# First tile of x in two loads, the mask fill behind the third tile, one more weight cast on ScalarE

## The chip, the cores and the metric

The kernel runs on one core of one Trainium2 chip. The metric is the device time of one execution in microseconds (us). Times inside the kernel come from one profiled execution; they are counted from the first instruction of the program on the core.

The engines are named as the profile names them: PE is TensorE (PEld its weight loads), DVE is VectorE, ACT is ScalarE, POOL is GpSimd and SP is SyncE, which here only issues loads and stores.

## What is computed

A graph attention layer on 384 nodes with 1024 features, and a quantised gated feed-forward network (FFN) behind it, both with a layer norm in front and a residual around:

```python
def _layernorm(x, axis=-1, eps=1e-05):
    m = jnp.mean(x, axis=axis, keepdims=True)
    v = jnp.var(x, axis=axis, keepdims=True)
    return (x - m) / jnp.sqrt(v + eps)
...
q = x @ wq.T + bq                       # the same for k and v, 1024 x 1024 each
q2 = (q @ wiq.T + biq).reshape(N, H, D).transpose(1, 0, 2)    # 16 heads of 64, the same for k2, v2
mask = _build_mask(edge_index, edge_type, edge_type_weights, x.dtype)   # -inf where no edge
scores = jnp.einsum('hnd,hmd->hnm', q2, k2) * scale + mask[None]
attn = jax.nn.softmax(scores, axis=-1)
out = jnp.einsum('hnm,hmd->hnd', attn, v2)
return out.transpose(1, 0, 2).reshape(N, OUT_F) @ wo.T + bo
...
def _weight_fake_quant(w):
    scale = jnp.max(jnp.abs(w), axis=1, keepdims=True) / QMAX
    return jnp.clip(_ste_round(w / scale), -QMAX - 1.0, QMAX) * scale
gate = jnp.einsum('bsh,ih->bsi', xq, _weight_fake_quant(w_gate))
up = jnp.einsum('bsh,ih->bsi', xq, _weight_fake_quant(w_up))
h = _act_fake_quant(jax.nn.silu(gate) * up, clip_down[0])
return jnp.einsum('bsi,hi->bsh', h, _weight_fake_quant(w_down))
...
x = x + gnn(_layernorm(x))
x = x + ffn(_layernorm(x))
```

The FFN has 352 inner units, so w_gate and w_up are 352 x 1024 and w_down is 1024 x 352.

## The kernel before

The 384 rows of x are three tiles of 128 (NT = 3), the 1024 features eight chunks of 128 (KC = 8). The matrix work is in 32-bit floats but for the FFN, whose quantised weights and inputs are exact in bf16.

**Order of the work.** PE, SP and POOL run their instructions in the order of the program text in the whole kernel. DVE and ACT do so in the first stage (line 280) and in the last (line 791); between them, in the attention stage, a scheduler sets their order when the kernel is compiled. Every engine works through its own list in order: an instruction that waits holds up all that is behind it.

**Start (lines 84 to 382).** SP issues the loads: tiles 0 and 1 of x (line 88), the first two blocks of wq (line 80), tile 2 of x, then further blocks of wq, wk and so on, one 512 KB load each. Weight blocks go into eight buffers, and each load also waits for the landing of the eighth load before it. PE begins with 36 transposes of a unit matrix (WARM, line 328) that nobody reads. For each tile t of x:

- `row_stats(t)` on DVE: two statistics of 512 columns (line 294), their merger (295), and the reciprocal of the standard deviation (lines 122 to 131, with a square root on ACT),
- `normalise(t)` on DVE: two halves of 512 columns (line 302),
- `turn(t, xn, g)` on PE: four transposes for each half (line 311), copied out of PSUM by ACT in pairs (line 315),
- `q_first(o, t)` on PE: the products of tile t with the first two blocks of wq (line 320), as soon as the chunks are there.

In the text the work runs: statistics, normalisation and turning of tile 0; then statistics and normalisation of tile 1; `q_first(0, 0)`, then part of `q_first(1, 0)`; turning of tile 1, and so on to tile 2.

**POOL at the start.** It makes the unit matrix, issues the loads of biases, edge weights, clip factors and edges, makes two index tables (lines 109 and 112), clears `w_scale` (149), and fills the mask, 128 x 3 x 384 floats, with the value that stands for "no edge" (151). Once DVE has made the edge keys (345), POOL writes them to DRAM (348) and issues three loads that spread them over all partitions (271). Later DVE puts the diagonal into the mask (411), POOL writes the mask to DRAM (415), and 51 indirect transfers put the edges in (450). Line 464 loads the finished mask back.

**Projections (lines 480 to 513).** Each pair of weight blocks takes seven products of four matmuls (`project2`, Strassen's scheme in Winograd's form), from about 22 to 159 us. The last inner products for k (`inner_k`) use the same function in the attention stage.

**Attention stage (lines 709 to 787).** For each of eight pairs of heads p: score products (line 651) with the mask added on DVE (657) and the exponential on ACT (661), the weighting of the pair before (`weigh`: transposes on line 681 into two PSUM buffers, copies by ACT on line 683, products on line 689), and, spread between them, filler products: `inner_v` (line 625) for even p, `inner_k` (line 203) for odd p. In `project2` a product goes into one of two PSUM buffers (pool `ps_mm`), and a buffer is free for the next product but one when DVE and ACT have read it (lines 217 to 238).

**FFN weights.** Into the same stage `ffn_weights` spreads the quantisation of 14 blocks of FFN weights (u = 0 to 13): three of w_gate, three of w_up, eight of w_down. For each block: the largest value of each row (527) and its reciprocal scale (528, 530) on DVE, scaling to 8-bit integers on ACT (533, one buffer `w8b`), a cast to bf16 into `wqi` (two buffers), then transposes on PE (570 or 580) and a copy on ACT. The cast is on ACT (537) for blocks u < 3 and on DVE (539) for the others. PE transposes into the same two PSUM buffers (`ps_tp`) as `weigh`. Block u = 3, the first of w_up, is quantised during pair p = 1, while `inner_k(2)` is the filler.

**End (from line 839).** Output projection, residual, layer norm, FFN and the stores.

Of the kernel before, what the change touches and what calls it, by code (L numbers as in the profile page):

```python
# [32 lines left out]
P = 128  # L33
N = 384
NT = N // P
F = 1024
# [18 lines left out]
NO_EDGE = -8e30  # L55


def row_bcast(ap, n):
    return bass.AP(tensor=ap.tensor, offset=ap.offset, ap=[[0, P], [1, n]])
# [3 lines left out]
def gnn_ffn_kernel(ctx: ExitStack, tc: tile.TileContext, a: dict, out: bass.AP):  # L63
    nc = tc.nc
# [13 lines left out]
    def load_w(name, j):  # L78
        wt = w.tile([P, F], F32, name="wt")
        nc.sync.dma_start(wt, a[name][j])  # L80
        return wt


    x = act.tile([P, NT, F], F32, name="actT")
    for t in range(NT):
        if t == NT - 1:
            wq_first = [load_w("wq", o) for o in range(FIRST)]
        nc.sync.dma_start(x[:, t, :], a["x"][t * P : (t + 1) * P, :])
    bias_rows = const.tile([5 * KC, P], F32)
    etw = const.tile([P, 4], F32)  # L90
    clip = const.tile([P, 2], F32)
# [55 lines left out]
    w_scale = ffn.tile([P, 2, 3], F32)  # L147
    wd_scale = ffn.tile([P, KC], F32)
    nc.gpsimd.memset(w_scale, 0.0)
    mask = ffn.tile([P, NT, N], F32)  # L150
    nc.gpsimd.memset(mask, NO_EDGE)
    sig = ffn.tile([P, 2], F32)
    per_max = ffn.tile([P, 5], F32)

# [105 lines left out]
    with ph1_stack:  # L260
# [6 lines left out]
        def load_keys():  # L267
            c0 = len(key_b) * 4 * GROUP
            part = ph1.tile([P, 4 * GROUP * P], F32, name="key_b", bufs=3)
            n = min(4 * GROUP, EC - c0) * P  # L270
            nc.gpsimd.dma_start(part[:, :n], row_bcast(key_row_d[:, c0 * P : c0 * P + n], n))
            key_b.append(part)
# [25 lines left out]
        def normalise(t):  # L298
            xn = rows_p.tile([P, F], F32, name="row")
            for j in range(2):  # L300
                hs = slice(j * 512, (j + 1) * 512)
                nc.vector.tensor_scalar(
                    xn[:, hs], x[:, t, hs], mv1[:, t, 0:1], rstd1[:, t : t + 1], op0=ALU.subtract, op1=ALU.mult
                )
            return xn
# [11 lines left out]
        def q_first(o, t, ks=range(KC)):  # L317
            ts = slice(t * P, (t + 1) * P)
            for k in ks:
                nc.tensor.matmul(  # L320
                    pm_first[o][:, ts], wq_first[o][:, k * P : (k + 1) * P], xnT[:, k, ts],
                    start=(k == 0), stop=(k == KC - 1),
                )
# [24 lines left out]
        nc.gpsimd.dma_start(key_row_d.rearrange("a (c p) -> (a c) p", p=P), key_row)  # L348
        for _ in range(3):
            load_keys()  # L350
        xn = normalise(2)
        q_first(0, 1)
        q_first(1, 1, range(6))
# [171 lines left out]
    def quantise_rows(wn, rows, n, scale, on_scalar=False, wq=None):  # L525
        mx = small.tile([P, 1], F32, name="wmx")
        nc.vector.tensor_reduce(mx[:rows], wn[:rows, :n], axis=AX.X, op=ALU.max, apply_absolute_value=True)
        nc.vector.tensor_scalar(scale, mx[:rows], 1.0 / QMAX, None, op0=ALU.mult)
        rs = small.tile([P, 1], F32, name="wrs")
        nc.vector.reciprocal(rs[:rows], scale)  # L530

        w8b = rows_p.tile([P, F], I8, name="w8b", bufs=1)
        nc.scalar.activation(w8b[:rows, :n], wn[:rows, :n], AF.Copy, scale=rs[:rows])
        if wq is None:
            wq = rows_p.tile([P, F], BF16, name="wqi", bufs=2)
        if on_scalar:
            nc.scalar.copy(wq[:rows, :n], w8b[:rows, :n])
        else:
            nc.vector.tensor_copy(wq[:rows, :n], w8b[:rows, :n])
        return wq  # L540

    def ffn_weights():

        units = [(name, m, ic) for m, name in enumerate(("L0_ffn_w_gate", "L0_ffn_w_up")) for ic in range(3)]
        units += [("L0_ffn_w_down", 2, c) for c in range(KC)]
        ahead = []

        def load_row():
            name, m, j = units[len(ahead)]
            i0, rows = ICS[j] if m < 2 else (j * P, P)  # L550
            wn = rows_p.tile([P, F], F32, name="row")
            nc.sync.dma_start(wn[:rows, : F if m < 2 else I], a[name][i0 : i0 + rows, :])
            ahead.append(wn)

        load_row()
        load_row()
        yield
        for u, (name, m, j) in enumerate(units):
            wn = ahead[u]
            if len(ahead) < len(units):  # L560
                load_row()
            if m < 2:
                i0, rows = ICS[j]
                wT = (wgT, wuT)[m]

                wq = quantise_rows(wn, rows, F, w_scale[:rows, m, j : j + 1], on_scalar=u < 3)
                yield
                pt = ps_tp.tile([P, KC, P], BF16, name="tp")
                for k in range(KC):
                    nc.tensor.transpose(pt[:, k, :rows], wq[:rows, k * P : (k + 1) * P], ident_b[:rows, :rows])  # L570
                nc.scalar.copy(wT[:, :, i0 : i0 + rows], pt[:, :, :rows])
            elif j >= KC - LATE:
                quantise_rows(wn, P, I, wd_scale[:, j : j + 1], wq=wd_late[:, j - KC + LATE, :])
                yield
            else:
                wq = quantise_rows(wn, P, I, wd_scale[:, j : j + 1])
                yield
                pt = ps_tp.tile([P, 3, P], BF16, name="tp")
                for ic, (i0, rows) in enumerate(ICS):
                    nc.tensor.transpose(pt[:rows, ic, :], wq[:, i0 : i0 + rows], ident_b)  # L580
                nc.scalar.copy(wdT[:, 0:2, j * P : (j + 1) * P], pt[:, 0:2, :])
                nc.scalar.copy(wdT[:96, 2, j * P : (j + 1) * P], pt[:96, 2, :])

    prep = ffn_weights()

    next(prep)
    nc.sync.dma_start(biv_b, row_bcast(a["L0_gnn_biv"], F))

    with ExitStack() as ph:
# [124 lines left out]
        for p in range(NP):  # L714
# [12 lines left out]
            if p == NP - 2:  # L727

                x = act.tile([P, NT, F], F32, name="actT")
# [143 lines left out]
    with ExitStack() as ph:  # L873
# [84 lines left out]
        for col, ic, c0, width in ((0, 0, 0, N), (1, 1, 0, N), (2, 2, 0, N // 2), (3, 2, N // 2, N // 2)):  # L958
            i0, rows = ICS[ic]
            cs = slice(c0, c0 + width)  # L960
# [118 lines left out]
```

## Time and profile before

| | us |
|---|---|
| median of 3 runs | 368.62 |
| the three runs | 368.3, 368.62, 368.91 |
| the profiled execution, whole | 368.32 |
| its span, first to last instruction | 366.5 |

| stage of the profiled execution, us from the start | PE busy | DVE busy | ACT busy | POOL busy |
|---|---|---|---|---|
| 0 to 9 | 9.00 | 4.61 | 2.50 | 6.46 |
| 9 to 23 | 14.00 | 12.20 | 7.55 | 2.37 |
| 182 to 189.4 | 6.79 | 7.22 | 5.07 | 0.00 |
| 189.4 to 194 | 4.60 | 2.13 | 3.11 | 0.00 |

The busy time of the first stage on PE contains the 36 warm-up transposes. The granted TensorE clock is 0.995 over the span and 1.00 in each of these stages.

How to read what follows. A line of the timeline has the start in us, the duration, engine, line of the kernel, operation, what it writes and reads, sizes, the count, and in brackets how long the engine was idle before it and what ended that. Neighbouring rows of one engine overlap a little, since an instruction begins while the one before it drains. The chain of waits gives start, share of the chain and line. A list of waits gives who waited for whom: total, times, longest.

### The profile page before, as it was taken

How to read it: one execution, taken by the hardware profiler on the slowest of the kernel's cores; microseconds unless marked ns; L12 is line 12 of the kernel's file. 1: busy time of each engine (PE TensorE's matmuls, PEld its weight loads, DVE VectorE, ACT ScalarE, POOL GpSimd, SP SyncE). 2: the span in 40 equal slices, each digit the busy share in tenths (PEclk: the TensorE clock that was granted, in tenths of full speed). 3: DMA queues.
4: the chain of work that ended last, by engine and by line, in shares of the span. 5: the costliest groups of instructions: out<-in, count | busy, mean ns of one | idle time of the engine just before them, and what ended most of it. 6: DMA issues, size and time to landing. Idle time of an engine off the chain costs nothing.

```text
span 366.5 us, 5805 instructions
## 1 busy us (share of the span) xinstructions
PE 354.5 (97%) x2094; PEld 296.5 (81%) x2094; DVE 253.7 (69%) x771; ACT 116.6 (32%) x270; POOL 75.0 (20%) x84
## 2 busy tenths in 40 slices
PE   7999999999999999999999999999999999999981
PEld 7999999999999999998877879686867445449760
DVE  5888888888889979966286755747494521098775
ACT  2342000000000002314472737454553522133730
POOL 7010355455444552340000000000000000000003
PEclk9999999999999999999999999999999999999998
DMA  7969433343333368711500610041694000000004
GB/s 235 399 232 398 135 116 115 118 137 116 115 115 117 115 197 252 230 19 47 157 20 2 209 62 20 11 146 35 215 397 159 39 0 2 0 0 0 3 1 172
DMA packets 17804, 44.50 MB, mean 121 GB/s; under 512 B 3262, under 2 KB 8400, under 8 KB 17392
## 3 DMA queue, kind: packets, MB, share of 16 engines
q1 hardware_dynamic: 15104, 39.46, 31.6%
q0 software_dynamic: 2672, 4.68, 4.2%
q8 instruction: 16, 0.26, 0.3%
q14 instruction: 12, 0.10, 0.1%
HBM read 41.91 MB, written 2.21 MB: 120 GB/s over the span
## 4 chain that ended last, share of the span: by engine, by line
PE 91%; DVE 5%; DMA 1%; ACT 1%; issue 0%; DVEq 0%; ACTq 0%
PE p L203 37%; PE mm L625 12%; PE mm L203 9%; PE sc L651 5%; PE sc L689 5%; PE tp L681 4%; PE mm L699 3%; PE sc L699 3%; PE mm L855 3%; PE mm L320 3%; PE sc L855 1%; DVE y L1018 1%; PE mm L965 1%; DMA actT<-in_x_dram 1%; PE x L965 1%; ACT x L949 1%
## 5 line engine op out<-in xcount | busy, mean ns | idle before, releaser
L450 POOL DMA_INDIRECT mask_d<-value,place x51 | 58.8, 1154 | 66.6 <-DVE place L447 45.6
L203 PE MATMUL p<-actT,wt 128*128 128x192 f32 x360 | 65.9, 326 | 0.0
L203 PEld LDWEIGHTS p<-actT,wt 128*128 128x128 f32 x360 | 59.6, 190 | 0.1
L625 PE MATMUL mm<-wt,actT 128*128 128x256 f32 x192 | 45.8, 384 | 0.0
L625 PEld LDWEIGHTS mm<-wt,actT 128*128 128x128 f32 x192 | 34.9, 190 | 7.8 <-issue 2.8
L661 ACT ACTIVATE e<-s,mn 128x384 f32<-128x384 f32 x48 | 29.0, 605 | 32.3 <-DVE mn L657 32.3
L823 POOL TENSOR_SCALAR minus<-row 128x1 f32<-128x1 f32 x3 | 0.7, 222 | 175.2 <-DVE row L820 175.2
L657 DVE CUSTOM_DVE_ANT_0 s<-sc,mask 128x384 f32<-128x384 f32 x48 | 24.6, 553 | 15.8 <-PE sc L651 15.8
L203 PE MATMUL p<-x_right,s 128*128 128x192 f32 x176 | 32.2, 326 | 0.0
L203 PE MATMUL p<-x_right,wt 128*128 128x192 f32 x176 | 32.2, 326 | 0.0
L203 PEld LDWEIGHTS p<-x_right,s 128*128 128x128 f32 x176 | 29.2, 190 | 0.0
L203 PEld LDWEIGHTS p<-x_right,wt 128*128 128x128 f32 x176 | 29.2, 190 | 0.0
L437 DVE SCALAR_TENSOR_TENSOR junk<-key_b,key,later 128x384 f32<-128x384 f32 (+3 forms) x51 | 27.5, 540 | 0.0
L683 ACT COPY eTs<-tp 128x384 f32<-128x384 f32 x48 | 20.5, 477 | 21.8 <-PE tp L681 21.7
L217 ACT COPY actT<-p 128x192 f32<-128x192 f32 x15 | 4.8, 319 | 63.3 <-PE p L203 63.3
L214 DVE SCALAR_TENSOR_TENSOR actT<-p,bias,actT 128x192 f32<-128x192 f32 x45 | 18.7, 416 | 8.3 <-PE p L203 4.5
L227 ACT ACTIVATE actT<-p,bias 128x192 f32<-128x192 f32 x15 | 6.3, 420 | 50.1 <-PE p L203 32.2
L681 PEld LDWEIGHTS tp<-ident,e 128*128 128x128 f32 x144 | 17.1, 141 | 4.5 <-issue 2.6
L651 PE MATMUL sc<-k,actT 64*128 64x384 f32 x96 | 20.1, 518 | 0.0
L681 PE MATMUL tp<-ident,e 128*128 128x128 f32 x144 | 19.7, 273 | 0.0
L203 PE MATMUL mm<-actT,wt 128*128 128x192 f32 x96 | 19.0, 330 | 0.0
L689 PE MATMUL sc<-eTs,actT 128*64 128x384 f32 x96 | 17.2, 494 | 0.0
(225 smaller groups left out, 583.5 us busy)
## 6 DMA issues: line engine op xcount, KB each, us to landing
wt<-in_wq_dram SPq DMA_DIRECT2D x8, 512.0 KB
wt<-in_wk_dram SPq DMA_DIRECT2D x8, 512.0 KB
wt<-in_wv_dram SPq DMA_DIRECT2D x8, 512.0 KB
wt<-in_wiq_dram SPq DMA_DIRECT2D x8, 512.0 KB
wt<-in_wik_dram SPq DMA_DIRECT2D x8, 512.0 KB
wt<-in_wiv_dram SPq DMA_DIRECT2D x8, 512.0 KB
wt<-in_wo_dram SPq DMA_DIRECT2D x8, 512.0 KB
actT<-in_x_dram SPq DMA_DIRECT2D x6, 512.0 KB
```

Of the source, the lines that this page charges most:

```text
L203: nc.tensor.matmul(z, left[:, k * P : (k + 1) * P], r[:, k, :], start=(k == 0), stop=(k == HK - 1))
L214: nc.vector.scalar_tensor_tensor(dst, z, b, with_, op0=ALU.add, op1=ALU.add)
L437: nc.vector.scalar_tensor_tensor(junk[:, :left], keys[:, (c - k0) * P : (c - k0) * P + left], key[:, c : c + 1], later[:, :left], op0=ALU. ...
L450: ins = nc.gpsimd.indirect_dma_start(out=mask_d, out_offset=bass.IndirectOffsetOnAxis(ap=place[:, c : c + 1], axis=0), in_=value[:, c : c ...
L625: nc.tensor.matmul(pm, vT[:, k, t * P : (t + 1) * P], wt[k // HK][:, k0 : k0 + 256], start=(k == 0), stop=(k == KC - 1),)
L651: nc.tensor.matmul(ps[t, h], q2[hs, t * P : (t + 1) * P], k2[hs, :], start=True, stop=True)
L657: taken.append(nc.vector.tensor_tensor_reduce(s, ps[t, h], mask[:, t, :], -SCALE, 3.0e38, op0=ALU.add, op1=ALU.min, accum_out=mn[h][:, t : ...
L661: nc.scalar.activation(e[h][:, t, :], s, AF.Exp, bias=mn[h][:, t : t + 1], scale=-1.0, accum_out=sm[h][:, t : t + 1],)
L681: nc.tensor.transpose(pt[:, t * P : (t + 1) * P], e[h][:, t, m * P : (m + 1) * P], ident)
L683: nc.scalar.copy(eT[h][m], pt)
L689: nc.tensor.matmul(pav[h * D : (h + 1) * D, :], v2[:, m, c0 : c0 + D], eT[h][m], start=(m == 0), stop=(m == NT - 1),)
L699: nc.tensor.matmul(pm, outT[:, k, t * P : (t + 1) * P], wo[k][:, gs], start=(k == 0), stop=(k == KC - 1))
```

## The change

Three edits. (1) Tile 0 of x is loaded by two transfers of 512 columns each instead of one of 1024. (2) The fill of the mask moves in POOL's list from behind the clearing of `w_scale` to behind the three key loads. (3) The cast of block u = 3 moves from DVE to ACT.

```diff
     for t in range(NT):
         if t == NT - 1:
             wq_first = [load_w("wq", o) for o in range(FIRST)]
-        nc.sync.dma_start(x[:, t, :], a["x"][t * P : (t + 1) * P, :])
+
+        for cs in (slice(0, 512), slice(512, F)) if t == 0 else (slice(0, F),):
+            nc.sync.dma_start(x[:, t, cs], a["x"][t * P : (t + 1) * P, cs])
...
     nc.gpsimd.memset(w_scale, 0.0)
     mask = ffn.tile([P, NT, N], F32)
-    nc.gpsimd.memset(mask, NO_EDGE)
...
         for _ in range(3):
             load_keys()
+        nc.gpsimd.memset(mask, NO_EDGE)
         xn = normalise(2)
...
-                wq = quantise_rows(wn, rows, F, w_scale[:rows, m, j : j + 1], on_scalar=u < 3)
+                wq = quantise_rows(wn, rows, F, w_scale[:rows, m, j : j + 1], on_scalar=u < 4)
```

In the compiled program the instructions of PE are the same in the same order. On DVE one cast of 128 x 1024 is gone, on ACT one is added, directly behind the first of the four exponentials that follow the block's scaling; the rest of both lists is in the order of before. SP has one transfer more.

## The prediction, made before the changed kernel ran

> **What bounds the kernel now.** I read the page's busy times first, then the chain that ended last, then the waits of TensorE alone, and last the timeline around each of its waits.
>
> ```profile
> PE 354.5 (97%) x2094; PEld 296.5 (81%) x2094; DVE 253.7 (69%) x771; ACT 116.6 (32%) x270; POOL 75.0 (20%) x84
> ...
> PE 91%; DVE 5%; DMA 1%; ACT 1%; issue 0%; DVEq 0%; ACTq 0%
> ```
>
> TensorE is busy for 354.5 of 366.5 us and carries 91% of the chain. An edit is worth what it does to TensorE's few waits. These are all of them (us in total, times, longest):
>
> ```profile
> PE mm L1014 <- DVE hq L1005: 1.6, 1, 1.6
> PE tp L328 <- POOL ident masks.py:199: 1.4, 1, 1.4
> PE mm L203 <- DVE k L220: 0.6, 1, 0.6
> PE tp L311 <- DVE row L302: 0.6, 1, 0.6
> PE mm L965 <- DVE xqT L951: 0.4, 2, 0.2
> ```
>
> The fourth is where the first two edits act, the third where the last one acts. Between 22 and 340 us that third wait is the only one, so a delay of TensorE there stays to the end, and so does a gain.
>
> The start, from the timeline (start, duration):
>
> ```profile
> 4.13 1.29 DVE L294 BATCH_NORM_STATS2 st<-actT 128x6 f32<-128x512 f32 x2 [3.24 <-DMA actT<-in_x_dram]
> ...
> 6.17 1.07 POOL L151 MEMSET mask<- 128x1152 f32 x1
> 6.68 1.30 DVE L302 TENSOR_SCALAR row<-actT,mv,rstd 128x512 f32<-128x512 f32 x2
> ...
> 7.59 1.17 PE L311 MATMUL tp<-ident,row 128*128 128x128 f32 x8 [0.58 <-DVE row L302]
> ...
> 10.43 1.00 DVE L302 TENSOR_SCALAR row<-actT,mv,rstd 128x512 f32<-128x512 f32 x2
> ```
>
> The same pair of L302 takes 1.30 us beside the mask fill and 1.00 without it.
>
> The middle, first the chain, then ScalarE's timeline:
>
> ```profile
> 187.92 0.61 DVE wqi L539
> 188.53 0.47 DVE s L657
> 189.00 0.28 DVE k L220
> 189.33 1.57 PE mm L203 x8
> 190.89 0.66 PE tp L681 x6
> ```
> ```profile
> 186.59 1.15 ACT L533 ACTIVATE w8b<-row,wrs 128x1024 int8<-128x1024 f32 x1 [1.66 <-DVE wrs L530]
> 187.64 0.60 ACT L661 ACTIVATE e<-s,mn 128x384 f32<-128x384 f32 x1
> ...
> 189.44 0.60 ACT L661 ACTIVATE e<-s,mn 128x384 f32<-128x384 f32 x1
> ...
> 190.04 0.82 ACT L683 COPY eTs<-tp 128x384 f32<-128x384 f32 x2
> ```
>
> The cast of the fourth block (L539, 0.61 us of the chain) stands in front of the k addition that TensorE waits for. ScalarE, into whose queue the cast goes, has no idle time from 186.59 to 190.86 either.
>
> **First tile in halves.** VectorE starts its two statistics when the whole tile has landed, at 4.13; the second starts at 4.74. After, the first half is through before the rest lands, and the second half's statistics start as it lands. If it lands when the whole did, they start 0.61 us sooner; if it lands one issue later (SP's first two issues take 0.86, so 0.43 each), 0.18. I take near the first: the second tile, issued 0.44 after the first, lands 1.24 after it by the DMA records (4.10, 5.34), so the data and not the issue sets landings. Packets of 2048 bytes take 84 ns against 159 for 4096, and each of 16 engines has eight rows: 8 x 9 ns = 0.07 later. VectorE gains 0.54. All later loads move back one place on SP; they run far ahead, but for the two below.
>
> **Mask fill moved.** The first tile's pair loses the 0.30 above. In its new place the fill follows the three key loads on POOL, whose issues end at 22.86, so it ends near 23.9. Its first reader, L411, runs at 32.40; behind it POOL has only the mask transfer at 33.84. The VectorE rows beside it (22.95 to 23.57) may be stretched by up to 0.30; VectorE then idles 1.46 before 25.03, which hides that. Without this cover it would be 0.30.
>
> **What of this reaches TensorE.** VectorE is 0.84 ahead (0.48 to 0.91). The warm-up transposes are not shortened: the last starts at 6.73, in steps of 0.11, so the first real one can come at 6.84 and not 7.59: at most 0.74. But then the weights are late. The first q block takes 16 matmul rows from 8.71; the second block's first row stands at 10.59, and its weights land only at 10.18 (SP's wait for them ends at 10.2, a semaphore row). That leaves 0.41, less 0.07 for the smaller packets, less 0.06 from release to start (189.27 to 189.33), less 0.10 for the restart (the step after a wait is 0.21, otherwise 0.11). **TensorE gains 0.2.** Bounds: 0.74 if the weights land early, and a loss of 0.18 if they land one SP issue (0.44) later. The third tile of x lands at 11.79 as before; its normalised half is ready at 16.02, and TensorE will want it at 16.2, so that holds.
>
> **Cast moved.** In the compiled order of both kernels the only difference here is that the cast leaves VectorE and stands on ScalarE behind the first of four exponentials; three exponentials, two L683 copies and the L227 bias wait behind it.
> - VectorE: k L220 ends 0.61 sooner (188.67), and TensorE's wait of 0.61 goes. Its product then ends early, and it reaches the transposes L681 at 190.13, not 190.73.
> - ScalarE: the three earlier casts on it (L537) take 1.03 to 1.05 us; neighbouring rows overlap by 0.09 (the copy at 174.85 lasts 0.99, the next row starts at 175.74), so the queue moves by 0.95. The two copies end at 191.44 and 191.81 instead of 190.49 and 190.86.
> - Those copies free the two PSUM buffers of the transposes. The first trio starts at 191.49, the second, 0.06 behind the second copy, at 191.87, against 191.06 before. **TensorE is 0.81 later than before**, after a wait of some 1.3 us in place of 0.6.
> - Late next: L227 about 0.8, which frees a buffer that TensorE wants 0.8 later too; the following copies end at 193.07, and the third group of transposes comes at 193.8. So nothing is added, and nothing given back. The cast's reader (L570 at 200.53) has 11 us.
> - Bounds for the cast on ScalarE: VectorE's 0.69 (0.60 of queue, +0.46) and the same block's L533, 1.15 (1.06, +0.92). I take 0.95, from the same operation on the same engine.
>
> The Trainium skill, page "ScalarE: Activation LUTs", section "Rules for kernel authors", speaks against this part: it sends plain elementwise work to VectorE and budgets about 0.3 us and 0.83 ns per element for an ACTIVATE. For 1024 elements that is an estimate of 1.15 us; with it the part would cost 0.92 and the sum be +0.7, where the rows of 1.04 give +0.6. The page "TensorE: Matmul & The Clock Gate", section "A second HAM failure mode: psum-queue depth-cycling", holds that frequent short idle times can drop the clock for a window of 3.4 us, an estimated 1.7 us more. This trace's clock stays at 1.00 in the stretch behind the 0.61 us wait; no row shows one of 1.3.
>
> **Sum.** 0.81 - 0.2 = +0.6 us. The profiled execution took 368.32 us, its span 366.5 and 1.8 around it; so 368.9 for that one. The median of the three runs is 0.3 above it: **369.2**, 0.17% slower. A measurement tells about 0.2%, 0.74 us, from no change.
>
> **Rivals.**
> - *The ScalarE wait takes the place of the VectorE wait, the start gives 0.2* (forecast, 0.60): 369.2, own range 368.7 to 369.5 (+0.1 to +0.9).
> - *The start gives nothing back* (0.20): the second weight block lands a place later, and the start costs 0.18: +0.99, 369.6. For it: one more issue ahead of it on SP. Against: the data rate above. It decides once the weights land after 10.43.
> - *The weights come early* (0.08): the start gives its whole 0.74: +0.07, 368.7. They would have to land by 9.7.
> - *ScalarE doesn't bind* (0.12), the other side: if the cast's block began about 1.4 us earlier, inside the 1.66 that ScalarE idles before 186.59, the copies would be in time, TensorE would keep the 0.61 and the 0.2, and the time be 367.8. It decides from there: less than 0.77 earlier and TensorE still loses. For it: the idle time is long enough. Against: it ends with VectorE's reciprocal L530 at 186.50, behind six multiplications of L671, and that order is unchanged.
>
> **The numbers.** Some two thirds of the forecast case lie below +0.74, 0.38, and the early weights add 0.08: within 0.2%, 0.46. The rest of it (0.22) and the second case (0.20) are slower: 0.42. Faster is the last case, 0.12. The range leaves that case out and the far end of the second: 368.5 to 369.7.
>
> **What would show it.** Right: TensorE waits over 1 us for the copies L683 at the second group of transposes, and its wait for k L220 is gone or below 0.2; the first transposes start near 6.9; a new wait of the second q block for the wq load; the first L302 pair at 1.0. Wrong: no wait at L681, or the exponentials running ahead of the cast; weights that land before 9.8 or after 10.5; a granted clock below 1 after 191 us.

## The result, and the profile after

| | before | after |
|---|---|---|
| median, run beside each other, us | 368.84 | 371.93 |
| lowest and highest, us | 368.27, 369.31 | 369.44, 374.01 |
| profiled execution, us | 368.32 | 372.07 |
| its span, us | 366.5 | 370.3 |

The ratio is 1.0074, 95% interval 1.0056 to 1.0092: slower by three quarters of a percent. The forecast was 369.2 us with a range of 368.5 to 369.7, so the result lies above the range. The spread is new as well: 4.6 us between the fastest and the slowest execution, against 1.0 before.

The busy times of the page, and the list of TensorE's waits (us in total, times, longest), both of the changed kernel:

```profile
PE 356.1 (96%) x2094; PEld 297.8 (80%) x2094; DVE 253.0 (68%) x770; ACT 117.5 (32%) x271; POOL 73.5 (20%) x84
```
```profile
PE mm L321 <- ACT u L124: 2.1, 1, 2.1
PE mm L1016 <- DVE hq L1007: 1.6, 1, 1.6
PE tp L329 <- POOL ident masks.py:199: 1.3, 1, 1.3
PE tp L683 <- ACT eTs L685: 1.2, 1, 1.2
```

Two lines are new. The last is the one that was predicted: TensorE's transposes wait 1.2 us for ScalarE's copies, and the wait of 0.6 for k is gone. The first was not: the first q product waits 2.1 us. It is put down to a small ScalarE instruction that merely ended last; the first wq block landed at 11.10 us (a semaphore row; 7.08 in the kernel before), and the product began at 11.23. In the table of stages ahead, PE's 9.00 us for 0 to 9 should read 7.07: TensorE starts at 1.35 and waits 0.58 in front of 7.59.

TensorE runs the same 2094 instructions in both kernels, so their starts can be laid side by side, and the difference says where time is lost:

| place | before, us | after, us | later by |
|---|---|---|---|
| first transposes | 7.59 | 8.08 | 0.49 |
| first q product | 8.71 | 11.23 | 2.53 |
| products at 143 to 147 us | 147.15 | 150.04 | 2.89 |
| behind the wait for k | 189.33 | 191.62 | 2.29 |
| second group of transposes | 190.73 | 194.38 | 3.65 |
| its end, and from there to the end | 191.17 | 194.93 | 3.76 |

So 2.5 us of the 3.8 are lost in the first 12 us, 0.87 at the cast (2.89 to 3.76), and 0.36 at 143 to 147 us. The 0.36 can't be put down to the change: the profile of the cast alone, which has the start of before, loses 0.36 at the same place, and those of the split alone (e1) and of the cast on GpSimd (e4) lose nothing there. Both profiles are of single executions; by the ratio of all executions the change costs 2.7 us.

**The start.** TensorE's first q product, before and after; then the chain of waits of the changed kernel, in order of time (start, duration), and VectorE's timeline:

```profile
8.71 3.39 PE L320 MATMUL mm<-actT,wt 128*128 128x128 f32 x28
```
```profile
11.23 3.36 PE L321 MATMUL mm<-actT,wt 128*128 128x128 f32 x28 [2.12 <-ACT u L124]
```

```profile
1.63 7.66 DMA actT<-in_x_dram
9.29 0.02 issue
9.32 1.30 DVE st L295 x2
...
11.23 0.80 PE mm L321 x5
```
```profile
3.46 1.46 DVE L295 BATCH_NORM_STATS2 st<-actT 128x6 f32<-128x512 f32 x2 [2.57 <-DMA actT<-in_x_dram]
...
6.18 1.00 DVE L303 TENSOR_SCALAR row<-actT,mv,rstd 128x512 f32<-128x512 f32 x2
9.32 1.29 DVE L295 BATCH_NORM_STATS2 st<-actT 128x6 f32<-128x512 f32 x2 [2.13 <-DMA actT<-in_x_dram]
```

Up to 7.2 us VectorE does what the two edits intended: its statistics begin on half a tile, the normalise pair takes 1.00 instead of 1.30 us, and it starts at 6.18 instead of 6.68. Then the second tile is missing. Its load was issued at 1.63 us instead of 1.17 and landed at 9.29 instead of 5.34: 0.46 us later in, 3.95 us later out. The first wq block behind it was issued 0.47 us later (2.10 instead of 1.63) and landed 4.02 us later (11.10 instead of 7.08), and that is what TensorE waits for. The chain runs through the second tile only because it follows the ScalarE instruction that ended last; the tile itself isn't late for TensorE, which turns it at 14.43 while its normalised halves are there at 12.86. The same shows in the windows of 3.5 to 8 us; the last three columns are granted clock, busy share of the DMA engines and GB/s, first before, then after:

```profile
3.50:8.00 4.50, 3.92 (x32) 3.69 (x30) 3.52 (x10) 0.29 (x1) 3.74 (x8) 1.00 0.99 277
```
```profile
3.50:8.00 4.50, 4.50 (x28) 4.50 (x27) 3.26 (x9) 0.29 (x1) 2.73 (x7) 1.00 0.89 198
```

The DMA engines are shown as busy for almost as long but move 198 GB/s instead of 277. The packet records say how: most 4096-byte packets take 159 ns in both kernels, but of the 209 on SP's queue that start between 3.3 and 8.0 us in the changed kernel 23 take 400 to 2333 ns, more than a third of all their packet time; before it is 2 of 318, at most 446.

**The middle.** ScalarE, then TensorE, changed kernel:

```profile
190.54 0.60 ACT L663 ACTIVATE e<-s,mn 128x384 f32<-128x384 f32 x1
...
191.14 1.03 ACT L539 CAST wqi<-w8b 128x1024 bf16<-128x1024 int8 x1
...
193.88 0.83 ACT L685 COPY eTs<-tp 128x384 f32<-128x384 f32 x2
```
```profile
191.62 1.57 PE L204 MATMUL mm<-actT,s 128*128 128x192 f32 x8
194.38 0.92 PE L683 MATMUL tp<-ident,e 128*128 128x128 f32 x6 [1.20 <-ACT eTs L685]
```

The cast stands behind the first exponential and takes 1.03 us, the copies come behind it, and the second group of transposes has nowhere to write until they are through.

### The profile page after: what moved, and what is told of

Its sections match the earlier page's. It is cut to its first block, busy times and chain, and to the rows that moved or that the text cites. A ratio compares the mean times of both kernels' runs of the same rounds, so it can differ in the third digit from the quotient of the medians.

```text
span 370.3 us, 5807 instructions
## 1 busy us (share of the span) xinstructions
PE 356.1 (96%) x2094; PEld 297.8 (80%) x2094; DVE 253.0 (68%) x770; ACT 117.5 (32%) x271; POOL 73.5 (20%) x84
## 3 DMA queue, kind: packets, MB, share of 16 engines
HBM read 41.91 MB, written 2.21 MB: 119 GB/s over the span
## 4 chain that ended last, share of the span: by engine, by line
PE 87%; DVE 4%; DMA 4%; ACT 2%; issue 1%; SPq 1%; DVEq 0%; ACTq 0%
PE p L204 34%; PE mm L627 12%; PE mm L204 9%; PE sc L653 5%; PE sc L691 5%; PE tp L683 4%; PE mm L701 3%; PE sc L701 3%; PE mm L857 3%; PE mm L321 3%; DMA actT<-in_x_dram 2%; DMA biv_b<-in_L_gnn_biv_dram 2%; PE sc L857 1%; DVE y L1020 1%; PE mm L967 1%; PE x L967 1%
## 5 line engine op out<-in xcount | busy, mean ns | idle before, releaser
L452 POOL DMA_INDIRECT mask_d<-value,place x51 | 57.3, 1124 | 67.6 <-DVE place L449 47.0
```

The costliest lines, as they stand in the source:

```text
L452: ins = nc.gpsimd.indirect_dma_start(out=mask_d, out_offset=bass.IndirectOffsetOnAxis(ap=place[:, c : c + 1], axis=0), in_=value[:, c : c ...
```

## The experiments

All edits are to the kernel before, unless it is said otherwise; none leaves out or changes part of the computation. Three questions: which edit costs what, what the freed VectorE wait was worth, and what happens to the second tile.

### Each edit alone

The split of the first tile alone (e1_split_only), the mask fill alone (e2_mask_only) and the cast alone (e3_cast_only): the three hunks of the diff above, one at a time.

> The kernel before with only the first tile of x loaded in two halves; mask fill and cast as before. Theory A (the two halves disturb the loads behind them: in the changed kernel's profile the second tile landed at 9.29 us instead of 5.34, the first wq block at 11.10 instead of 7.08): slower by 1.5 to 3 us with a wider spread than before, second tile landing after 6.5 us, TensorE's first q product at 10 us or later. Rival B (the loads are late because the mask fill no longer stands where it stood on GpSimd): within 0.5 us of before, second tile by 5.7 us. Rival C (chance of one execution, and the whole loss is in the cast): faster by 0.1 to 0.3 us.

> The kernel before with only the mask fill moved behind the key loads. Theory A: the first pair of normalisations takes 1.00 us instead of 1.30, TensorE's first q product comes 0.3 us sooner, the weights of the second q block (landed at 10.18) leave that room, so faster by 0.2 to 0.3 us. Rival B (the fill's place disturbs the loads): slower by 1 to 3 us.

> The kernel before with only the cast of the fourth block on ScalarE. Theory A (ScalarE's queue takes the place of the wait on VectorE): TensorE waits about 1.2 us for the copies at the second group of transposes, the wait of 0.61 us on k is gone, slower by 0.8 us (0.7 to 1.0). Rival C (whole loss of the change is here): slower by 2 us or more. Rival D (the scheduler's order makes it free): faster by 0.6.

| | time, us | before beside it | ratio | 95% interval |
|---|---|---|---|---|
| split alone | 371.1 | 368.9 | 1.0052 | 1.0030 to 1.0074 |
| mask fill alone | 368.95 | 368.9 | 1.0006 | 0.9996 to 1.0015 |
| cast alone | 369.61 | 368.9 | 1.0020 | 1.0011 to 1.0030 |

The three sum to 0.78%, and all together give 0.74%: they add up within their intervals, and the split carries two thirds. The cast alone shows in its profile the wait of 1.2 us at the transposes, and TensorE 0.86 later there.

The mask fill alone brings TensorE's first transposes to 7.25 us instead of 7.59, but the 0.2 to 0.3 us that were expected don't show in the time. In its profile the lead is gone at 143 us, behind a wait of VectorE for the load of an FFN weight block (landed at 138.42 us, 138.30 in the profile of before). That the lead is lost because this load doesn't come sooner is not shown: the cast alone, with no lead, loses 0.36 there as well.

The split alone also shows a second cost, in its windows (span of the window, then busy time and instructions of PE, PEld, DVE, ACT and POOL, then clock, DMA share, GB/s):

```profile
8.00:11.00 3.00, 0.79 (x8) 0.48 (x6) 1.65 (x4) 1.38 (x5) 0.00 (x0) 1.00 0.99 371
11.00:14.40 3.40, 3.40 (x16) 3.40 (x17) 2.29 (x7) 0.12 (x1) 0.00 (x0) 0.50 1.03 413
14.40:20.00 5.60, 5.60 (x52) 5.60 (x52) 2.62 (x10) 1.49 (x5) 0.28 (x1) 1.00 0.88 347
```

```profile
10.97 4.99 PE L321 MATMUL mm<-actT,wt 128*128 128x128 f32 x28 [2.21 <-DMA wt<-in_wq_dram]
```

Here the wait is put down to the weights themselves. TensorE works only 0.79 us of the 3.00 before 11.0, and then the granted clock is 0.50 for 3.41 us: the same 28 matmuls that took 3.36 us in the changed kernel's profile took 4.99. In that profile the wait was as long (2.12 us against 2.21) and the clock stayed at 1.00. So a wait of this length costs another 1.6 us in some executions and nothing in others. The mean granted clocks of the executions agree: in the changed kernel the five of 372.36 to 374.01 us have 0.988 to 0.992 and the seven of 369.44 to 372.07 us have 0.993 to 0.997; in the split alone the five of 372.19 us and more have 0.989 to 0.990, the six of 371.10 us and less 0.993 to 0.996. The clock thus goes with the upper half of the spread; the 2.6 us among the other seven stay unexplained.

### What the freed wait was worth

e4_cast_pool gives the cast of the fourth block to GpSimd, which is idle there, so that neither VectorE nor ScalarE has it:

```diff
+        if on_pool:
+            nc.gpsimd.tensor_copy(wq[:rows, :n], w8b[:rows, :n])
...
+                wq = quantise_rows(..., on_scalar=u < 3, on_pool=u == 3)
```

> The kernel before with the cast of the fourth block on GpSimd, which has no other work in that stage, and so in no queue that TensorE waits for. Theory A: VectorE is 0.6 us earlier at the k addition, TensorE's wait of 0.61 us goes and none takes its place: faster by 0.5 to 0.6 us. Rival (GpSimd's reads and writes slow VectorE's instructions beside it): within 0.2 us of before.

368.82 us beside 368.9, ratio 0.9999 (0.9989 to 1.0008): nothing. Its TensorE timeline:

```profile
189.31 1.57 PE L203 MATMUL mm<-actT,s 128*128 128x192 f32 x8
191.13 0.92 PE L683 MATMUL tp<-ident,e 128*128 128x128 f32 x6 [0.26 <-ACT eTs L685]
```

The wait for k is gone, and the transposes behind it wait for the copies instead. In this profile TensorE comes to this place 0.60 us later than in that of before, is 0.02 sooner once the wait for k is gone, and 0.40 to 0.51 later again 2 us on: of 0.62 us, 0.1 to 0.2 are kept. So the copies stood right behind the k addition: taking the cast off VectorE, with nothing put on ScalarE, earns 0.1 to 0.2 us here and not its 0.61, and the expectation of half a microsecond was wrong.

### The second tile: number, size or time of issue

First, how the first tile is cut and from which queue. e5_rows cuts it into two halves of rows, so that every packet keeps its 4096 bytes; e6_second and e8_third cut the second or the third tile into column halves instead; e7_actq issues the second column half from ScalarE's queue.

```diff
 e5   for r0, r1 in ((0, 64), (64, P)) if t == 0 else ((0, P),):
          nc.sync.dma_start(x[r0:r1, t, :], a["x"][t * P + r0 : t * P + r1, :])
 e6   ... if t == 1 else ...
 e8   ... if t == 2 else ...
 e7   (nc.scalar if cs.start else nc.sync).dma_start(x[:, t, cs], ...)
```

> The kernel before with the first tile of x loaded in two halves of rows (64 partitions each, rows of 4096 bytes as before) instead of one load: one transfer more ahead of the second tile, no smaller packets. Theory number (one more transfer in front is what holds up the second tile): second tile lands after 7 us, first wq block after 9 us, slower by 1.5 to 2.5 us like the halves of columns. Theory size (rows of 2048 bytes are what holds it up): second tile by 5.7 us, first wq block by 7.5 us, time within 0.5 us of before.

> The kernel before with the second tile of x loaded in two halves of columns, the first in one. Theory size: the loads behind the halves, the first two wq blocks, are held up (first wq block after 8.5 us instead of 7.1), slower by 1 to 2.5 us. Theory number: the same. Theory place (only the very first transfers of the program suffer, since the first rows are read slowly): first wq block by 7.6 us, within 0.5 us of before.

> The first tile of x in two halves of columns, the second half issued from ScalarE's queue at the same time as SP issues the first. Theory size: both halves land by 4.3 us, but the second tile is held up past 7 us as with both on SP; slower by 1.5 to 2.5 us. Theory number on one queue (SP's queue has one transfer more ahead of the second tile): with SP's list as long as before the second tile lands by 5.7 us; time within 0.5 us of before.

> The kernel before with the third tile of x in two halves of columns: the first four transfers are as before. Every theory: second tile by 5.7 us and first wq block by 7.6 us as before; the third tile lands within 0.5 us of its 11.8; time within 0.4 us of before. If it is slower by 1 us or more, the halves disturb the loads whatever their place.

| | time, us | ratio | 95% interval |
|---|---|---|---|
| e5, halves of rows | 371.71 | 1.0069 | 1.0042 to 1.0097 |
| e6, second tile | 369.37 | 1.0010 | 0.9997 to 1.0022 |
| e7, ScalarE's queue | 368.84 | 0.9996 | 0.9984 to 1.0008 |
| e8, third tile | 368.89 | 1.0003 | 0.9992 to 1.0015 |

Small packets are not needed for it: e5 is as bad with packets of 4096 bytes. It is no clean test, since its halves are slower themselves (the second landed at 5.43, and the second tile was issued only at 1.98); e13 below, which keeps every transfer of before, settles this. Cutting as such isn't the cause either (e8, e7). In e7's profile, its highest time of ten (369.48 us), the second tile landed at 5.33, but the first weight block at 9.43, and the first q product began 0.86 us later than before; its median shows no loss. In e6 the second half of the second tile is the one that is issued at 1.63; it landed at 6.34, and the first weight block at 9.53 instead of 7.08: the same delay in a milder form, behind the tile that is wanted first. None of its expectations had this: the weights are as late as 'number' said, the time is within the half microsecond of 'place'. What the bad ones share is one more issue on SP ahead of the second tile.

e12_count makes only that: 960 and 64 columns instead of 512 and 512. e9_after_actq is the changed kernel, all three edits in it, with the second half issued from ScalarE's queue.

> The first tile in two transfers of 960 and 64 columns, nothing else changed: one transfer more on SP's queue, and nearly the same packets as before. Theory 'third transfer on the queue is slow, whatever came before': the second tile again falls to half the rate and lands near 9, time 370.5 to 371.5. Rival 'bytes': the second tile lands at 5.3 to 5.8 and the time is that of before, 368.9.

> The changed kernel with one edit: the second half of the first tile is issued from ScalarE's queue, the mask fill and the cast stay moved. Theory 'place on SP's queue': the start's loss (2.5 us of the changed kernel's 3.8) goes, only the cast's is left: the second tile lands near 5.3 instead of 9.29, the time is 369.3 to 370.0, about that of the cast alone (369.61). Rival 'two halves are slow beside the moved fill': the second tile still lands after 8 and the time stays above 371.

e12 took 371.72 us, ratio 1.0079 (1.0056 to 1.0103): a transfer of 32 KB costs as much as a half tile, though the second tile landed at 7.67 in its profile (the lowest time of four, 369.46 us) and not near 9. e9 took 369.99, ratio 1.0027 (1.0016 to 1.0039), where the changed kernel has 1.0074: moving that one issue off SP takes back 0.47%, or 1.7 us, and leaves the cast's loss, just inside the range expected. TensorE's timeline in e9 shows that the start isn't clean there either; the second tile landed at 5.32, but the first weight block at 9.84:

```profile
7.75 1.04 PE L312 MATMUL tp<-ident,row 128*128 128x128 f32 x8
9.97 3.36 PE L321 MATMUL mm<-actT,wt 128*128 128x128 f32 x28 [1.18 <-DMA wt<-in_wq_dram]
```

Up to here the theory was that the number of transfers on SP's queue counts. e13_delay separates it from its rival, the time of issue: VectorE first fills the second tile's place, SP has to wait for that, and no transfer is added.

```diff
+        if t == 1:
+            nc.vector.memset(x[:, 1, :], 0.0)
         nc.sync.dma_start(x[:, t, :], a["x"][t * P : (t + 1) * P, :])
```

> The kernel before with one fill of the second tile's place by VectorE (128 x 1024 zeros, overwritten by the load) ahead of the second tile's load: SP must wait for it, so the second tile and all loads behind it are issued some 0.4 to 0.5 us later, with no transfer added. Theory 'number of transfers on the queue': the queue keeps its rate beyond 3.5 us, the second tile lands at 5.3 to 6.0, the time is 368.8 to 369.4. Rival 'time of issue': the rate falls to 200 KB per us at 3.5 us, the second tile lands beyond 7.5 and the time is above 370.5.

371.01 us, ratio 1.0066 (1.0037 to 1.0095). The theory of the number falls. The chain at its start:

```profile
1.01 0.91 DVE actT L89
...
1.96 0.32 SPq L90
...
2.33 7.97 DMA wt<-in_wq_dram
```

The second tile is issued at 1.95 us instead of 1.17 (0.78 later, where 0.4 to 0.5 were expected) and lands at 8.94, the first weight block at 10.30, though SP has exactly the transfers of before. The fill ends at 1.92, before that load is issued, and the first tile lands at 4.06, as before.

Two more things are under way in those microseconds: GpSimd's seven small loads (biases, edge weights, two clip factors, three of edges; issued from 1.46 to 5.5 us; the expectations count six), and the weight loads behind the second tile. Three kernels, all on top of the split: e11_split_late issues the small loads 1.5 us later (from 2.96 us); e15_small_gated only when the second tile has landed; e16_weights_held lets SP go on to the weights only when the first tile has landed. A copy of one column ahead of the small loads (e15) or of the first wq load (e16) makes them wait.

```diff
 e15
+    nc.gpsimd.tensor_copy(landed, x[:, 1, F - 1 :])
 e16
+            nc.vector.tensor_copy(wt[:, :1], after)
...
+            wq_first = [load_w("wq", o, x[:, 0, F - 1 :] if o == 0 else None) for o in range(FIRST)]
```

> The split alone, with GpSimd's six small loads (biases, edge weights, clip factors, edges) issued some 2 us later, behind the index tables and the mask fill. Theory 'the small loads slow the queue': the bytes of SP's queue keep coming at some 390 KB per us beyond 3.5 us, the second tile lands at 5.3 to 6.5 and the first weight block before 9, time 369.5 or less. Rival 'the place on SP's queue alone': the rate falls to 200 KB per us at 3.5 us as before, the second tile lands at 9 or later, time near 371.

> The split alone, with a one-column copy by GpSimd out of the second tile ahead of its six small loads, so that it issues them only once the second tile has landed. Theory 'a late issue alone': the rate on SP's queue still falls at 3.5 us to some 200 KB per us, and the second tile lands beyond 7. Rival 'the small loads of GpSimd': the rate stays near 390 KB per us until the second tile has landed at 5.3 to 5.8.

> The split alone, with a one-column copy by VectorE out of the first tile into the place of the first weight block ahead of its load, so that SP issues the weights and all behind them only when the first tile has landed (4.2 us). Theory 'a late issue alone': the second tile is issued as late as with the split and lands beyond 7, the weights beyond 10. Rival 'the loads issued behind it hold it up': with nothing behind it the second tile lands at 5.3 to 5.8, and the weights some 3 us after 4.4.

All that bears on the question, from the DMA and semaphore records of the profiles; the KB columns are what the queues of SP and ScalarE had moved by then, and the last two the median time and that of the profiled execution:

| kernel | 2nd tile issued, us | landed | 1st wq block landed | KB by 3.5 us | 5.0 | 6.5 | median, us | profiled, us |
|---|---|---|---|---|---|---|---|---|
| before | 1.17 | 5.34 | 7.08 | 476 | 1048 | 1604 | 368.84 | 368.32 |
| e9, with ScalarE's queue | 1.17 | 5.32 | 9.84 | 478 | 1048 | 1372 | 369.99 | 370.79 |
| after | 1.63 | 9.29 | 11.10 | 476 | 780 | 1064 | 371.93 | 372.07 |
| e12, 960 + 64 columns | 1.63 | 7.67 | 9.42 | 471 | 772 | 1160 | 371.72 | 369.46 |
| e5, halves of rows | 1.98 | 10.39 | 11.85 | 304 | 576 | 844 | 371.71 | 374.5 |
| e13, late issue | 1.95 | 8.94 | 10.30 | 500 | 724 | 916 | 371.01 | 371.01 |
| e11, small loads later | 1.63 | 7.73 | 9.09 | 488 | 652 | 1088 | 370.12 | 369.8 |
| e15, small loads behind it | 1.63 | 7.63 | 8.91 | 466 | 752 | 1196 | 374.01 | 373.25 |
| e16, weights held | 1.63 | 6.48 | 11.29 | 504 | 860 | 1024 | 369.95 | 372.74 |

The two tiles are 1024 KB. The rows that issue the second tile at 1.17 have 1048 KB by 5.0 us; those that issue it at 1.63 or later have 576 to 860. The rate drops as the second tile comes up, and neither the small loads (e15) nor the weights behind it (e16) are needed for that; both taken away at once was not tried. That they prolong it is likely but not shown. For it: in e15 the rate is back to some 400 KB per us from 6.0 us on (1020 KB at 6.0, 1816 at 8.0), where the changed kernel moves from 980 to 1316 KB in the same time; and with nothing behind it the second tile lands at 6.48 (e16), which lies between theory and rival, as e11 does. Against it: e12, which has both, landed its second tile at 7.67, no later than e11 and e15. The times of e15 and e16 hold other delays too, of GpSimd's work and of the weights, and are not read for this.

Each landing is of one profiled execution; e15 ran twice, e12 four times, e5 and e13 five times. The four further kernels whose first loads are those of before (e2, e3, e4, e8) tell how far landings scatter: second tile 5.41 to 5.49, first weight block 7.13 to 8.37. The second tiles that were issued late, from 6.34 (e6, its second half) to 10.39, are all outside that. The weights are not as clear: in e7 and e9 the first block is issued at 1.63, as before, and lands at 9.43 and 9.84, in e10 at 7.84. What holds them up there, with the second half on another queue, was not tested.

### Versions that could beat both

e10_mask_actq has the mask moved and the second half on ScalarE's queue, and no cast moved. e14_wq_actq issues the first weight block from that queue as well:

```diff
+            wq_first = [load_w("wq", o, nc.scalar if o == 0 else None) for o in range(FIRST)]
```

> The first two edits with the second half issued from ScalarE's queue, without the cast. Theory 'place on SP's queue', with the weights as the next wait: the first transposes start up to 0.7 sooner but the first q product waits for the weights, so 368.4 to 368.9, at best 0.1% under before. Rival 'the start can be given away': 368.1 or less, 0.2% under before.

> The first two edits, with the second half of the first tile and the first weight block both issued from ScalarE's queue, and no cast moved. Theory 'two queues side by side': the first weight block is the second transfer of its queue and lands by 7.5, the first q product follows the first transposes at once, 368.3 to 368.7. Rival 'the queues share the engines and the second tile is held up': it lands beyond 7 and the time is 369.2 or more.

368.77 us, ratio 0.9995 (0.9984 to 1.0007), and 368.68, ratio 0.9993 (0.9980 to 1.0006): no difference that can be told from none. In e14 the weights are in time (landed at 7.32 us; the second tile, which shares the time with them, at 6.77), as TensorE's timeline shows, and still the start isn't sooner than before:

```profile
1.34 6.42 PE L329 MATMUL tp<-ident 128*128 128x128 f32 x36 [1.34 <-POOL ident masks.py:199]
7.60 1.04 PE L312 MATMUL tp<-ident,row 128*128 128x128 f32 x8
8.66 3.39 PE L321 MATMUL mm<-actT,wt 128*128 128x128 f32 x28
```

The first normalised half is there at about 7.1 us, but the 36 warm-up transposes last 6.42 us here, against 5.66 in the profile of before. A warm-up step takes 0.21 us until the full clock is granted and 0.11 after, and the grant came at 6.04 us here, at 4.49 in that of before.

## Why the prediction was wrong

**Where it failed: the place on SP.** The step is in "First tile in halves": "so the data and not the issue sets landings", and from it "All later loads move back one place on SP; they run far ahead, but for the two below". The observation behind it was right, tile 1 did land 1.24 us after tile 0 though it was issued 0.44 after. What it didn't carry is that the landing stays put when the issue moves. 0.46 us of issue made 3.95 us of landing in the changed kernel, 0.78 us made 3.60 in e13, and the weights followed. In the changed kernel the first wq block was issued 0.47 us later and landed 4.02 later, at 11.10, and TensorE waited 2.1 us for it. With that the start costs 2.5 us in this profile (0.52%, 1.9 us, by the split alone) instead of gaining 0.2, and the bound of that gain, a loss of 0.18 "if they land one SP issue (0.44) later", was worked out by the same step: it shifted the landing by the issue, one for one. Of the weights only the second block was asked about; the first, which TensorE came to wait for, and the second tile ahead of it were not.

**The rival that had the right sign.** "The start gives nothing back" named the weights a place later in SP's list, with "one more issue ahead of it on SP" for it. It had the right place and the wrong size: the weights landed at 11.10 (first block) and 12.42 (second), beyond its 10.43, and the start cost 2.5 us and not 0.18.

**VectorE's gains were right.** Predicted 0.54 for the statistics, measured 0.50 (they end at 4.92 instead of 5.42); predicted 0.30 for the normalise pair, measured 0.30; the pair ends 0.80 us sooner, against 0.84. They were gains in front of a wait.

**The first transposes at 6.84.** They came at 8.08. The cap was taken from the warm-up transposes of one profile, where the full clock came at 4.49 us. In the changed kernel's it came at 7.02, and over the profiles here from 4.17 to 7.42, with no order by edit. So the place where the warm-ups end is no constant, and VectorE's lead at this point is worth 0.3 in one execution and nothing in the next.

**The mask fill.** Right in price (0.30) and in that its new place is covered; that its lead of 0.3 shows in no time (ratio 1.0006) was not foreseen, and where it goes is not shown.

**The cast was right.** Cast 1.03 us (predicted 1.03 to 1.05), wait at the second group of transposes 1.2 (some 1.3), TensorE later by 0.87 in the changed kernel and 0.86 in the cast alone (0.81). The rival in which ScalarE doesn't bind, 367.8 us, needed the copies to be out of the way; e4 shows that even with no cast on ScalarE they take most of the 0.61 back.

**The clock behind the new wait.** It stays at 1.00 from 191 to 197 us after the wait of 1.2, as the trace of before suggested. At the start the clock did fall, in the split alone, behind a wait of 2.21 us with little work before it. The Trainium skill, page "TensorE: Matmul & The Clock Gate", section "Why this matters for your kernels", warns of idle gaps over some 3 us; the runs here show a drop behind a shorter one, and none behind another of the same length (2.12 us, changed kernel).

**Open.** Why a load that is issued half a microsecond later finds the queue at half its rate is not settled. Shown is that, with the transfers of before, the time of issue alone makes the second tile late (e13), and that the packets' size, the number of transfers, the small loads and the loads behind it are not, each by itself, what starts it. Not shown is what the last two add, and why the first weight block was late in e7 and e9 though it was issued as before.

## What to carry to other kernels

An issue is not hidden because its queue "runs far ahead": look at how long before its turn each load is issued, and if something is put in front of the first loads of a kernel, price every load behind it, not only the one that is wanted sooner. A second engine's queue is the cheap way out: the same two halves cost 0.5% from one queue and, in the median of ten executions, nothing from two (ratio 0.9996). And before an engine is relieved of work that a wait ends on, ask what ends second: here it stood 0.1 to 0.2 us behind, so nothing was to be had, while the engine that took the work over came a full microsecond late with work that TensorE waited for.

## What the hardware showed that was not expected

- Half a microsecond of issue cost up to four of landing: issued at 1.17 us the second tile landed at 5.34, issued at 1.63 between 7.6 and 9.3 (6.48 with the weights held back). The Trainium skill, page "DMA: Bandwidth & Descriptors", section "Rules for kernel authors", says that spreading transfers over several issuing engines saves only their issue time. That agrees with what was moved here, 0.46 us; the runs show that this much issue time was worth 1.7 us in e9.
- In the profile of before, the broadcast of 16 bytes to 128 partitions (edge weights, 16 packets of 128 bytes) takes 0.7 to 1.7 us for 14 of the 16 packets, between 6.3 and 8.4 us; SP's queue moves 112 KB from 6.5 to 8.0 us, where it moved 556 in the 1.5 us before.
- The grant of the full clock at the start came between 4.17 and 7.42 us in the profiles here, for the same warm-up. When it fell, it did so for 3.41 us (split alone, e15, e16) or 6.83 us (halves of rows).
